# Sparse graph attention: units of at most four slots, stages one step apart, weighting on ScalarE

## The chip, the cores and the metric

One core of a Trainium2 chip. The metric is the device time of one execution in microseconds (us), median of several runs. All runs told here were in the fast state. A ratio is the mean time of one kernel's fast runs over the mean of the other's of the same rounds, so it is not quite the ratio of the medians that stand beside it. Engines: PE is TensorE, DVE is VectorE, ACT is ScalarE, POOL is GpSimd.

## The reference, cut to what matters

```python
# x (16, 1024, 512); adj (1024, 1024), a few neighbours per row; 8 heads of 64
h = maximum(layernorm(x), 0)
q, k, v = (h @ W + b for each of the three)          # (B, N, 8, 64)
scores  = einsum("bihd,bjhd->bhij", q, k) / sqrt(64) + where(adj == 0, -1e9, 0)
out     = x + einsum("bhij,bjhd->bihd", softmax(scores), v)
```

The adjacency is the same for all 16 batches and sparse, so the kernel makes lists of neighbours once. Rows are sorted by their number of neighbours; a tile is 128 sorted rows, and a tile of short rows needs few slots. Per slot, one indirect DMA gathers a neighbour's k and v for 128 rows (512 KB).

## The kernel before: what the argument touches

One "unit" is a few slots of one tile: (tile, first slot, slots). Tile -1 holds the overflow pieces of the longest rows.

```python
UNITS = ((7,0,2), (6,0,3), (5,0,4), (4,0,4), (3,0,5), (2,0,6), (1,0,4), (1,4,4), (0,0,6), (-1,0,5), (0,6,5))
gpool = pool("gpool", 3)                  # gathered units
ON_ACT, BY_REDUCE = (0, 1, 2), (5, 8, 9)  # weighted by ACT; summed over slots by DVE
# ... cut ...
def ahead(n):                             # one tile of projections, for the next batch
    if n + 3 < tiles: load_x(n + 3)       # indirect DMA, issued by POOL
    if n + 2 < tiles: stats(n + 2)        # DVE, with a power on POOL
    if n + 1 < tiles: flip(n + 1)         # PE transposes
    proj_kv(n)                            # 2 x 4 matmuls, bias on DVE, store
    if n + 2 < tiles: norm(n + 2)         # ACT
# ... cut: the loop over units i ...
    score(i)                              # DVE: k*q, reduce, mask; ACT: exp
    if i: weigh(i - 1)                    # DVE or ACT: v*w
    go_ahead(...)                         # some ahead(n)
    if new tile: queries(nb, nt)
    if i: add_up(i - 1)                   # PE: sum of the slots by identity matmuls
    if i + 2 < total: gather(i + 2)       # POOL
    # at a tile's end: finish(...)        # DVE: divide; POOL: + x, store
```

All four engines run in exactly the written order.

Of the kernel before, what the change touches and what calls it, by code (L numbers as in the profile page):

```python
# [38 lines left out]
CAPS = (11, 8, 6, 5, 4, 4, 3, 2)  # L39
PIECE = 5  # L40
PIECES = 17
LIST = CAPS[0] + PIECE * PIECES

UNITS = ((7, 0, 2), (6, 0, 3), (5, 0, 4), (4, 0, 4), (3, 0, 5), (2, 0, 6), (1, 0, 4), (1, 4, 4), (0, 0, 6), (-1, 0, 5), (0, 6, 5))
UMAX = max(n for _, _, n in UNITS)
SLOTS = sum(n for _, _, n in UNITS)


def main_path(tc, x, adj, Wq, bq, Wk, bk, Wv, bv, out, sums, cover):
# [11 lines left out]
    with ExitStack() as ctx:  # L61
        pool = lambda name, bufs=1, **k: ctx.enter_context(tc.tile_pool(name=name, bufs=bufs, **k))
        const = pool("const")
        xpool = pool("xpool", 14)
        hpool = pool("hpool", 2)
        htpool = pool("htpool", 12)
        kvpool = pool("kvpool", 3)
        gpool = pool("gpool", 3)
        work = pool("work", 2)
        small = pool("small", 4)  # L70
        wpool = pool("wpool", 3)
# [6 lines left out]
        ps_n = pool("ps_n", 1, space=psum)  # L78
# [12 lines left out]
        rows = gpool.tile([P, 5, N], F32, tag="g", name="rows")  # L91
        iota, key_row, rank_row, from_end, junk = (rows[:, k, :] for k in range(5))
# [97 lines left out]
        def proj_kv(n):  # L190
            b, t = tile_at(n)
            if b not in KV:
                KV[b] = dram.tile([N, 2 * D], F32, tag="kv", name=f"kv_{b}")
            kv = kvpool.tile([P, 2, D], F32, tag="kvt", name=f"kvt_{b}_{t}")
            for j, name in enumerate("kv"):
                pt = ps_kv.tile([P, D], F32, tag="pkv", name=f"p{name}_{b}_{t}")
                project(pt, name, n)
                nc.vector.tensor_tensor(kv[:, j, :], pt, bias[name], ALU.add)
            nc.sync.dma_start(KV[b][ts(t, P), :], kv.rearrange("p j d -> p (j d)"))
# [7 lines left out]
        for tile_, first, count in UNITS:  # L207
            first_col[tile_, first] = col
            col += count
# [10 lines left out]
        def make_lists():  # L220
            nc.vector.tensor_scalar(from_end, rank_row, -1.0, float(N), op0=ALU.mult, op1=ALU.add)
            adj_p = [adj_tile(f"adj_sorted_{g}") for g in range(NT // 4)]
            for t in range(NT):
                row = adj_p[t // 4][:, t % 4, :]
                nc.gpsimd.indirect_dma_start(out=row, out_offset=None, in_=adj, in_offset=on(ap=perm[:, t : t + 1], axis=0))
                nc.vector.scalar_tensor_tensor(row, row, 0.0, from_end, op0=ALU.not_equal, op1=ALU.mult)
                if t:
                    found = small.tile([P, 8], F32, tag="found", name=f"found_{t}")
                    nc.vector.max(found, row)
                    spread(t, found)  # L230

            row = adj_p[0][:, 0, :]
            found = const.tile([P, LIST + 1], F32, tag="found0", name="found_0")
            for k in range(LIST // 8):
                nc.vector.max(found[:, ts(k, 8)], row)
                if k < LIST // 8 - 1:
                    nc.vector.match_replace(row, found[:, ts(k, 8)], row, 0.0)
# [7 lines left out]
            before = ps_n.tile([P, 1], F32, tag="n", name="p_before")  # L245
# [12 lines left out]
            p_list = ps_n.tile([P, width], F32, tag="n", name="p_list")  # L258
# [24 lines left out]
        Q, G, WT, ACC = {}, {}, {}, {}  # L283

        def queries(b, t):
            pt = ps_q.tile([P, D], F32, tag="q", name=f"pq_{b}_{t}")
            if t >= 0:
                project(pt, "q", nth(b, t))
                HT.pop(nth(b, t))
            else:  # L290
                nc.tensor.matmul(pt, owner, Q[b, 0], start=True, stop=True)
                Q[b, t] = pt
                return
            if t == 0:
                q = Q[b, t] = work.tile([P, D], F32, tag="q0", name=f"q0_{b}")
            else:
                q = Q[b, t] = pt
            nc.vector.tensor_tensor(q, pt, bias["q"], ALU.add)

        def gather(i):  # L300
            b, u = divmod(i, NU)
            t, first, count = UNITS[u]
            c = first_col[t, first]
            G[i] = gpool.tile([P, UMAX, 2, D], F32, tag="g", name=f"g_{b}_{u}")
            for s in range(count):
                nc.gpsimd.indirect_dma_start(  # L306
                    out=G[i][:, s].rearrange("p j d -> p (j d)"),
                    out_offset=None,
                    in_=KV[b][:],
                    in_offset=on(ap=index[:, c + s : c + s + 1], axis=0),  # L310
                )

        def score(i):
            b, u = divmod(i, NU)
            t, first, count = UNITS[u]
            c = first_col[t, first]
            k = G[i][:, :count, 0, :]
            nc.vector.tensor_tensor(k, k, Q[b, t][:, None, :].to_broadcast([P, count, D]), ALU.mult)  # L318
            if first == 0:
                WT[b, t] = wpool.tile([P, CAPS[t] if t >= 0 else PIECE, H], F32, tag="w" if t else "w0", name=f"w_{b}_{t}")  # L320
            w = WT[b, t][:, first : first + count, :]
            nc.vector.tensor_reduce(w, k.rearrange("p s (h d) -> p s h d", h=H), AX.X, ALU.add)  # L322
            nc.vector.tensor_tensor(w, w, mask[:, c : c + count, None].to_broadcast([P, count, H]), ALU.add)  # L323
            nc.scalar.activation(w, w, AF.Exp, scale=HD**-0.5)  # L324

        ON_ACT = (0, 1, 2)

        def weigh(i):
            b, u = divmod(i, NU)
            t, first, count = UNITS[u]  # L330
            v = G[i][:, :count, 1, :].rearrange("p s (h d) -> p s h d", h=H)
            w = WT[b, t][:, first : first + count, :]
            if u in ON_ACT:
                for s in range(count):
                    for h in range(H):
                        nc.scalar.mul(v[:, s, h, :], v[:, s, h, :], w[:, s, h : h + 1])  # L336
            else:
                nc.vector.tensor_tensor(v, v, w[:, :, :, None].to_broadcast([P, count, H, HD]), ALU.mult)  # L338

        BY_REDUCE = (5, 8, 9)  # L340

        def add_up(i):

            b, u = divmod(i, NU)
            t, first, count = UNITS[u]
# [5 lines left out]
            acc = ACC[b, home]  # L351
            if u in BY_REDUCE:
                r = work.tile([P, D], F32, tag="r", name=f"r_{b}_{u}")
                nc.vector.tensor_reduce(r, v.rearrange("p s d -> p d s"), AX.X, ALU.add)  # L354
                terms = [r]
            else:
                terms = [v[:, s, :] for s in range(count)]
            for k, term in enumerate(terms):
                nc.tensor.matmul(  # L359
                    acc,  # L360
                    owner_t if t < 0 else ident,
                    term,
                    start=(u == units[0] and k == 0),
                    stop=(u == units[-1] and k == len(terms) - 1),
                )

        def finish(b, t):
            s = sums[:, b * NT + t, :]
            nc.vector.tensor_reduce(s, WT.pop((b, t)).rearrange("p s h -> p h s"), AX.X, ALU.add)  # L369
            if t == 0:  # L370
                more = small.tile([P, H], F32, tag="more", name=f"more_{b}")
                nc.vector.tensor_reduce(more, WT.pop((b, -1)).rearrange("p s h -> p h s"), AX.X, ALU.add)
                pt = ps_n.tile([P, H], F32, tag="n", name=f"p_more_{b}")
# [18 lines left out]
        tiles = B * NT  # L392
        done = [0]

        def ahead(n):

            if n + 3 < tiles:
                load_x(n + 3)
            if n + 2 < tiles:
                stats(n + 2)  # L400
            if n + 1 < tiles:
                flip(n + 1)
            proj_kv(n)
            if n + 2 < tiles:
                norm(n + 2)

        def go_ahead(target):
            while done[0] < min(tiles, target):
                ahead(done[0])
                done[0] += 1  # L410
# [3 lines left out]
        for n in range(min(2, tiles)):  # L414
            stats(n)
            norm(n)
        flip(0)
        make_lists()
        LEAD = 2
        with tc.manual_schedule(engines={mybir.EngineType.PE, mybir.EngineType.DVE, mybir.EngineType.Activation, mybir.EngineType.Pool}):  # L420
            go_ahead(NT + LEAD)
            total = B * NU
            gather(0)
            gather(1)
            queries(0, UNITS[0][0])
            passed = 0
            for i in range(total):
                b, u = divmod(i, NU)
                if u == 0:
                    passed = 0  # L430
                passed += UNITS[u][2]
                score(i)
                if i:
                    weigh(i - 1)
                go_ahead(NT * (b + 1) + LEAD + NT * passed // SLOTS)
                if i + 1 < total:
                    nb, nu = divmod(i + 1, NU)
                    nt = UNITS[nu][0]
                    if (nb, nt) not in Q:
                        queries(nb, nt)  # L440
                if i:
                    add_up(i - 1)
                if i + 2 < total:
                    gather(i + 2)
                if i:
                    pb, pu = divmod(i - 1, NU)
                    home = max(UNITS[pu][0], 0)
                    if pu == NU - 1 or max(UNITS[pu + 1][0], 0) != home:
                        finish(pb, home)
            weigh(total - 1)  # L450
            add_up(total - 1)
            finish(B - 1, 0)
# [188 lines left out]
```

## Time and profile before

| | before |
|---|---|
| time, median of 3 runs | 2871.07 us (2868.92 to 2874.26) |
| busy: PE, DVE, ACT, POOL | 72%, 75%, 17%, 51% |
| first multiply of the first batch | 194 us |
| one batch | 166.7 us |
| mean granted clock of PE | 0.866 |

```profile
DMA to landing us min/median/max: 3.3/4.6/7.4
```

POOL issues a load at 597.0; the statistics at 600.4 belong to the tile loaded one step earlier, and those at 631.0 are the first to read this load:

```profile
596.99 0.97 POOL L154 DMA_INDIRECT x<-in_x_dram,perm  x1 [0.30 <-issue]
```

```profile
600.36 0.69 DVE L163 BATCH_NORM_STATS2 st<-x 128x6 f32<-128x512 f32 x1
...
630.99 0.68 DVE L163 BATCH_NORM_STATS2 st<-x 128x6 f32<-128x512 f32 x1
```

### The profile page before, as it was taken

The page shows a single profiled execution, that of the slowest core. Times are in us where ns is not written, and L with a number is a line of the kernel's source. Part 1 is how long each engine was busy: PE and PEld are TensorE (multiplying, and loading weights), DVE is VectorE, ACT ScalarE, POOL GpSimd, SP SyncE. Part 2 cuts the span into 40 slices and gives each one's busy share as a digit, 9 for nine tenths or more (in the row PEclk, how much of TensorE's full clock was granted, in tenths as well). Part 3 has the DMA queues.
Part 4 walks back from the last instruction along what each step waited for, and adds up shares of the span by engine and source line. Part 5 has one row for each costly group of instructions (what it writes and reads, how often), then busy time and mean ns, then how long its engine had stood idle before and what let it go on. Part 6 is the DMA issues. An engine that isn't in the chain of part 4 may idle for free.

```text
span 2872.0 us, 16724 instructions
## 1 busy us (share of the span) xinstructions
PE 2074.3 (72%) x4759; PEld 912.0 (32%) x4759; DVE 2161.5 (75%) x2287; ACT 485.2 (17%) x1590; POOL 1462.3 (51%) x1298
## 2 busy tenths in 40 slices
PE   0587786876779687677968767796876779687552
PEld 0233332332334233233423323342332334233211
DVE  8447868687786868778687877878687777867766
ACT  0012030301203030120303012030301203020110
POOL 2125455464555546455554655455464645645452
PEclk9998898888989888888989888897988889798776
DMA  5146565564656556465655656565564656556452
GB/s 186 48 149 217 189 228 197 176 216 169 220 195 227 201 176 217 167 222 194 230 198 181 228 174 219 183 226 200 185 225 169 221 180 231 199 185 216 152 188 81
DMA packets 153922, 550.40 MB, mean 192 GB/s; under 512 B 18784, under 2 KB 18784, under 8 KB 153824
## 3 DMA queue, kind: packets, MB, share of 16 engines
q0 software_dynamic: 132224, 474.02, 49.3%
q1 hardware_dynamic: 21600, 75.24, 6.5%
q8 instruction: 40, 0.66, 0.1%
q14 instruction: 58, 0.48, 0.1%
HBM read 448.53 MB, written 100.66 MB: 191 GB/s over the span
## 4 chain that ended last, share of the span: by engine, by line
PE 43%; DVE 36%; issue 8%; ACT 6%; DMA 6%; POOL 1%; DVEq 0%; SPq 0%; ACTq 0%; POOLq 0%
PE acc L359 13%; PE pq L188 10%; PE pk L188 9%; PE pv L188 8%; DVE g L318 8%; DVE r L354 8%; DVE w L322 7%; DVE g L338 5%; ACT g L336 5%; DMA g<-kv,index 5%; PE pht L182 2%; DVE w L323 1%; POOL g L306 1%; DVE st L163 1%; ACT h L175 1%
## 5 line engine op out<-in xcount | busy, mean ns | idle before, releaser
L306 POOL DMA_INDIRECT g<-kv,index x768 | 865.9, 1127 | 988.1 <-PE acc L359 418.1
L359 PE MATMUL acc<-g,ident 128*128 128x512 f32 x992 | 500.4, 646 | 111.0 <-ACT g L336 64.5
L188 PE MATMUL pk<-wk,hT 128*128 128x512 f32 x1024 | 497.2, 631 | 0.0
L188 PE MATMUL pq<-wq,hT 128*128 128x512 f32 x1024 | 489.1, 623 | 0.0
L188 PE MATMUL pv<-wv,hT 128*128 128x512 f32 x1024 | 460.3, 592 | 0.0
L359 PE MATMUL acc<-r,ident 128*128 128x512 f32 x64 | 65.9, 1133 | 460.4 <-DVE sums L369 242.3
L322 DVE TENSOR_REDUCE w<-g 128x32 f32<-128x2048 f32 (+4 forms) x160 | 391.4, 2446 | 5.5
L359 PEld LDWEIGHTS acc<-g,ident 128*128 128x128 f32 x992 | 193.9, 203 | 388.7 <-issue 206.6
L338 DVE TENSOR_TENSOR g<-g,w 128x2048 f32<-128x2048 f32 (+2 forms) x112 | 306.9, 2740 | 0.0
L324 ACT ACTIVATE w<-w 128x32 f32<-128x32 f32 (+4 forms) x160 | 37.0, 231 | 1566.0 <-DVE w L323 1566.0
L318 DVE TENSOR_TENSOR g<-g,pq 128x2048 f32<-128x2048 f32 (+4 forms) x128 | 291.5, 2278 | 0.1
L188 PEld LDWEIGHTS pq<-wq,hT 128*128 128x128 f32 x1024 | 206.7, 203 | 265.7 <-issue 262.6
L336 ACT ACTIVATE g<-g,w 128x64 f32<-128x64 f32 x1152 | 280.0, 333 | 0.6 <-ACT w L324 0.2
L188 PEld LDWEIGHTS pv<-wv,hT 128*128 128x128 f32 x1024 | 194.6, 190 | 244.9 <-issue 241.3
L188 PEld LDWEIGHTS pk<-wk,hT 128*128 128x128 f32 x1024 | 204.3, 211 | 205.7 <-issue 205.7
L381 DVE TENSOR_TENSOR o<-acc,inv 128x512 f32<-128x512 f32 x128 | 88.6, 692 | 226.2 <-PE acc L359 223.8
L354 DVE TENSOR_REDUCE r<-g 128x512 f32<-128x3072 f32 (+1 forms) x48 | 241.9, 5039 | 0.6
L387 POOL DMA_INDIRECT out_dram<-o,perm x128 | 207.6, 1622 | 37.3 <-POOL o L386 35.3
L166 POOL TENSOR_TENSOR rstd<-rstd,minus_half 128x1 f32<-128x1 f32 x128 | 74.1, 579 | 259.2 <-DVE rstd L165 257.2
L175 ACT ACTIVATE h<-x,shift,rstd 128x512 f32<-128x512 f32 x128 | 104.0, 813 | 545.1 <-issue 439.7
L386 POOL TENSOR_TENSOR o<-o,x 128x512 f32<-128x512 f32 x128 | 164.6, 1286 | 37.5 <-DVE o L381 34.6
L359 PEld LDWEIGHTS acc<-r,ident 128*128 128x128 f32 x64 | 16.0, 311 | 486.3 <-issue 294.8
(218 smaller groups left out, 1415.3 us busy)
## 6 DMA issues: line engine op xcount, KB each, us to landing
kv<-kvt SPq DMA_DIRECT2D x128, 512.0 KB, 4.0
g<-kv,index POOLq DMA_INDIRECT x768, 5.7
adj<-in_adj_dram SPq DMA_DIRECT2D x8, 512.0 KB, 7.1
x<-in_x_dram,perm POOLq DMA_INDIRECT x128, 4.6
out_dram<-o,perm POOLq DMA_INDIRECT x128, 4.6
wk<-in_L_gnn_Wk_dram SPq DMA_DIRECT2D x1, 1024.0 KB, 11.7
wv<-in_L_gnn_Wv_dram SPq DMA_DIRECT2D x1, 1024.0 KB, 13.0
wq<-in_L_gnn_Wq_dram SPq DMA_DIRECT2D x1, 1024.0 KB, 12.4
```

What stands on the lines that cost most here:

```text
L175: nc.scalar.activation(HN[n], X[n], AF.Relu, bias=shift, scale=rstd)
L188: nc.tensor.matmul(pt, HT[n][:, c, :], W[name][:, c, :], start=(c == 0), stop=(c == DC - 1))
L306: nc.gpsimd.indirect_dma_start(out=G[i][:, s].rearrange("p j d -> p (j d)"), out_offset=None, in_=KV[b][:], in_offset=on(ap=index[:, c + s ...
L318: nc.vector.tensor_tensor(k, k, Q[b, t][:, None, :].to_broadcast([P, count, D]), ALU.mult)
L322: nc.vector.tensor_reduce(w, k.rearrange("p s (h d) -> p s h d", h=H), AX.X, ALU.add)
L336: nc.scalar.mul(v[:, s, h, :], v[:, s, h, :], w[:, s, h : h + 1])
L338: nc.vector.tensor_tensor(v, v, w[:, :, :, None].to_broadcast([P, count, H, HD]), ALU.mult)
L354: nc.vector.tensor_reduce(r, v.rearrange("p s d -> p d s"), AX.X, ALU.add)
L359: nc.tensor.matmul(acc, owner_t if t < 0 else ident, term, start=(u == units[0] and k == 0), stop=(u == units[-1] and k == len(terms) - 1),)
L381: nc.vector.tensor_mul(o.rearrange("p (h d) -> p h d", h=H), ACC.pop((b, t)).rearrange("p (h d) -> p h d", h=H), inv[:, :, None].to_broadc ...
L386: nc.gpsimd.tensor_tensor(o, o, X.pop(nth(b, t)), ALU.add)
L387: nc.gpsimd.indirect_dma_start(out=out_rows, out_offset=on(ap=perm[:, t : t + 1], axis=0), in_=o[:], in_offset=None, element_offset=b * N * D)
```

## The change

The intent: shorten DVE's work (no long reductions over slots, most of the weighting on ACT), and break the turn-taking between DVE and PE by smaller units, more buffers, and stages that lie one step apart. The core of the diff, with some lines joined:

```diff
+UNITS = ((7,0,2), (6,0,3), (5,0,4), (4,0,4), (3,0,3), (3,3,2), (2,0,3), (2,3,3), (1,0,4), (1,4,4),
+         (0,0,4), (-1,0,4), (0,4,4), (0,8,4))      # written in one column in the file
+BY_VECTOR = (10, 11, 12)
-        gpool = pool("gpool", 3)
+        gpool = pool("gpool", 5)
... cut: lists run beside the first projections; k and v halves of a tile apart ...
+        scores = ps_w.tile([P, SLOTS, H], F32, tag="w", name="scores")        # PSUM
+        weights = const.tile([P, SLOTS, H], F32, tag="weights", name="weights")
... cut: score(i) reduces into scores, adds the mask, exponential into weights, then ...
+            if i % NU in BY_VECTOR:
+                nc.scalar.activation(sc, sc, AF.Exp, scale=HD**-0.5)
+            else:
+                v = heads(G[i][:, :count, 1, :])
+                for s in range(count):
+                    for h in range(H):
+                        nc.scalar.activation(v[:, s, h, :], v[:, s, h, :], AF.Identity, scale=weights[:, c + s, h : h + 1])
+        def weigh(i):
+            if i % NU in BY_VECTOR:
+                nc.vector.tensor_tensor(heads(v), heads(v), scores[:, w, :, None]..., ALU.mult)
+            if count == 4 and b < B - 1:
+                nc.vector.tensor_tensor(v[:, 0:2], v[:, 0:2], v[:, 2:4], ALU.add)      # the pair addition
... cut ...
+        def pending(h):                      # h counts halves: n is the tile, j = 0 for k and 1 for v
+            n, j = divmod(h, 2)
+            before, after = [], []
+            if j == 0:
+                if n + 2 < tiles: before.append((stats, n + 2))
+                if n + 1 < tiles: before.append((flip, n + 1))
+            else:
+                if n + 3 < tiles: before.append((load_x, n + 3))
+                if n + 2 < tiles: after.append((norm, n + 2))
+            return before, after
... cut: the loop over units i ...
+                if i + 3 < total: gather(i + 3)
+                if i: weigh(i - 1)
+                for k, h in enumerate(todo):      # 0 to 2 halves of projections in a step
+                    before, after = pending(h)
+                    run(before); proj_kv(*divmod(h, 2))
+                    if k == 0: multiply(i)
+                    elif k == 1: score(i)
+                    store_kv(*divmod(h, 2)); run(after)
+                ...
+                if i: add_up(i - 1)
+                if len(todo) < 2: score(i)
+                ... bias of q; finish of the tile that ended one step earlier
```

## The prediction

> **What bounds the kernel now.** I read the page's busy times first, then the chain, then the stretches of one batch, the waits and the timeline.
>
> ```profile
> PE 2074.3 (72%) x4759; PEld 912.0 (32%) x4759; DVE 2161.5 (75%) x2287; ACT 485.2 (17%) x1590; POOL 1462.3 (51%) x1298
> ...
> PE 43%; DVE 36%; issue 8%; ACT 6%; DMA 6%; POOL 1%; DVEq 0%; SPq 0%; ACTq 0%; POOLq 0%
> ```
>
> No engine is full, and the chain passes between PE and DVE: they take turns. The table of stretches has busy time of PE, weight loads, DVE, ACT, POOL, then clock, DMA share, GB/s; one batch is this:
>
> ```profile
> 411.00:579.00 168.00, 127.68 (x291) 56.39 (x290) 127.34 (x133) 29.65 (x98) 91.32 (x79) 0.86 0.57 195
> ```
>
> DVE stands idle 41 us of a batch, PE 40, ACT 138; DMA is at 57%. The timeline of DVE gives the period, from the first multiply of a batch to the next:
>
> ```profile
> 194.25 1.22 DVE L318 TENSOR_TENSOR g<-g,pq 128x1024 f32<-128x1024 f32 x1
> ...
> 351.06 1.21 DVE L318 TENSOR_TENSOR g<-g,pq 128x1024 f32<-128x1024 f32 x1
> ...
> 2685.12 1.21 DVE L318 TENSOR_TENSOR g<-g,pq 128x1024 f32<-128x1024 f32 x1
> ```
>
> So: 194 us of preparation, a first batch of 157, then (2685.1-351.1)/14 = 166.7 each, and 187 for the last batch with the end. The waits say who takes turns (us, times, longest):
>
> ```profile
> PE acc L359 <- DVE r L354: 307.5, 32, 19.5
> ...
> PE acc L359 <- DVE sums L369: 242.3, 16, 15.2
> ...
> DVE o L381 <- PE acc L359: 223.8, 97, 8.0
> DVE shift L173 <- POOL rstd L166: 131.6, 75, 4.6
> ```
>
> PE waits 550 us for the long DVE reductions of units of 5 and 6 slots, DVE 224 for sums that PE makes late in the same step. One step in the timeline:
>
> ```profile
> 610.12 1.27 POOL L386 TENSOR_TENSOR o<-o,x 128x512 f32<-128x512 f32 x1
> 610.35 1.09 DVE L323 TENSOR_TENSOR w<-w,mask 128x32 f32<-128x32 f32 x1
> ...
> 614.75 5.33 DVE L354 TENSOR_REDUCE r<-g 128x512 f32<-128x3072 f32 x1
> ...
> 620.22 2.05 PE L359 MATMUL acc<-r,ident 128*128 128x512 f32 x2 [15.15 <-DVE sums L369]
> ...
> 622.91 5.11 PE L188 MATMUL pk<-wk,hT 128*128 128x512 f32 x8
> ...
> 627.86 3.60 PE L188 MATMUL pv<-wv,hT 128*128 128x512 f32 x8
> ```
>
> PE waits 15 us for the reduction and then runs its next group in 5.11 us rather than 3.60; the mask addition takes 1.09 us while POOL adds.
>
> **What the Trainium skill says.** "SBUF — State Buffer", Who interferes with whom: a DVE instruction with two SBUF inputs contends with a GpSimd instruction that reads SBUF, one with at most one such input doesn't. The trace agrees: the mask addition of 32 columns has a mean of 928 ns, the longer one of 48, beside which POOL rarely adds, 208. "TensorE: Matmul & The Clock Gate", What's actually happening: after an idle window of about 3.4 us PE runs at half clock until it has been busy as long. The trace agrees (5.11 against 3.60 above; mean clock 0.86). "ScalarE: Activation LUTs", What ACT_TABLE_LOAD costs: 186 ns + 0.833 per element + 93 for a pointer operand, with 93 overlapped: 239 ns for 64 elements with a pointer scale. Measured: 32 of them in 7.73 us, 242 each. "PSUM — Partial Sum Buffer", PSUM bank collisions: two engines must not be in one bank at a time. All scores now lie in one bank, and in the built order each score reduction waits for the exponential of the unit before.
>
> **The change part by part, per batch.** DVE now: multiplies 48 slots, 27.7 (2.28 for four, 1.75 for three, 1.21 for two); score reductions as much; mask 14 x 0.2 = 2.8; k/v bias 16 x 0.69 = 11.0; q bias 5.6; statistics 8 x 1.18 = 9.4; finishing 10.9. These stay. Removed: the three sums over slots (5.33+5.33+4.46 = 15.1) and the weighting of 39 slots on DVE, of which 12 stay (3 x 2.28 = 6.9 against 21.7 now). Added: eight additions of slot pairs, 1.21 each by the multiply of 1024 elements, 9.7. The mask stall goes (scores in PSUM leave one SBUF input): 64 x 0.73 = 47 us in 16 batches, 3. So DVE falls from 129 to about 112.
> ACT: weighting goes from 9 slots to 36, 288 x 0.242 = 69.6 instead of 17.4: about 85 busy in all.
> PE: 32 sums instead of 34, else the same: 24 groups of four projections x 3.44 = 82.6, 33 x 0.86 = 28, transposes 7: 118 at full clock.
> POOL and DMA: the same 48 gathers; five buffers, and gathers three units ahead instead of two, so the DMA wait of 3 us at each "-1" unit goes.
>
> If only DVE's work counted, a batch would take 120. But a unit of four is added in pairs only when ACT has weighted all four, and in the built order that addition stands first in the next step, ahead of the next multiply. From the end of the mask addition to the pair addition lie 0.25 (exponential) + 7.73 + 0.1 = 8.1 us; DVE has only bias, finishing or a store to put in between. I walk through one batch, DVE in its built order:
> Units 0 and 1 (two and three slots, no pair addition) wait for PE instead: pair addition of unit 13, two sums (3.4 after its cold gap), pv 5, q 3.4, sums of unit 0, then the small product for the last tile: finishing ends at 16.
> Unit 2: 1.0 statistics + 2.3 + 0.7 + 2.3 + 0.2 = 6.5, then q bias and finishing 2.1, then wait 6.0: its pair addition begins at 31.
> Unit 3: 1.2 + 2.3 + 0.8 + 2.3 + 0.2 + 8.1 (2.1 of it used) = 15: 46.
> Units 4 to 7, no pair addition: 8.0 + 4.7 + 7.4 + 9 (some of it waiting for pv and pk, as PE stood idle some 9 us until unit 3 was added): 75.
> Unit 8: multiply, two stores, statistics, reduction 8.2, wait 7.3 after the last store: 91.
> Unit 9: 15 again, wait 6.1: 106.
> Units 10, 11, 12, weighted by DVE, no wait for ACT: pair addition 1.2 + 7.3, then 3.5 (weighting and pair) + 8.7 with a finishing, 3.5 + 7.3, 3.5: 141 (PE keeps up).
> Unit 13: 1.0 + 2.3 + 0.7 + 2.3 + 0.2 + 8.1 = 14.6: 156 and round again.
> Of that DVE waits 33 us for ACT in five places and some 10 for PE.
>
> Preparation: lists run beside the projections of batch 0. DVE per tile: three list steps of 2.6, two stores, statistics, shift, and 1.2 of waiting for pk: 11.6, for 6.7 tiles, 9.3 after that. First tile at 65, +78 = 143, pieces 5, gather and landing 8: first multiply at 156 instead of 194.
> Batch 0 takes 23 halves of projections instead of 16 (PE +24, DVE +9): 165. Batches 1 to 13: 13 x 156 = 2028. Batch 14 runs out of projections in its last four units: 149. Batch 15 has no pair additions; the exponentials queue behind ACT's weighting (70 us), and three units on DVE follow: 105. The end, from the last finishing on: 16.5 as now.
> Sum: 156 + 165 + 2028 + 149 + 105 + 17 = 2620 us, 9% less.
>
> **The rivals.** (a) PE or DVE becomes the bound and the stages overlap as meant: a period of 120 to 135, 2110 to 2330 in all. For it: both have that little work. Against it: the built order puts DVE's pair addition behind ACT's 8 us, and DVE is in order. (b) The new waits eat everything: cold PE after each of the three long gaps, POOL delayed by two-input pair additions, waits for scores in their one bank: 165 or more a batch, 2740 and up. Against it: DVE loses 17 us of work, the 15 us reductions' waits on PE shrink to 9, and the exponentials in my walk come before the reductions that need them, except in the last batch. (c) DMA: 33 MB in 156 us is 215 GB/s, under the 230 that slices of the page show now, and a gather has some 30 us until it is used: hidden.
>
> **Range and chances.** One us of the period is 14 us in all. My walk may be off by 6 us in a period, as it has about a dozen hand-overs between engines of 0.1 to 0.2 that I rounded, and cold PE that I placed by hand; preparation and end by 20. So 2520 to 2710. Faster by over 2% (under 2814): 0.96; same: 0.03; slower: 0.01.
>
> **What would show it.** DVE waiting for ACT's weighting before the pair addition, 70 to 80 times by about 6 us, some 490 in all (33 x 15), as the longest wait of DVE; POOL's statistics wait and the DMA wait near zero; the mask addition at 0.2; DVE busy near 112 per batch, ACT near 85; PE still under full clock (0.85 to 0.92). First multiply near 156. If DVE's wait for ACT is small, the walk is wrong and (a) holds; if PE waits end most of DVE's idle time, (b).

## More of the kernel before

The waits for x in the kernel before (us, times, longest) are one line of 1.6 us; the view of the x tiles ends with the time from a load's issue to its landing:

```profile
DVE st L163 <- DMA x<-in_x_dram,perm: 1.6, 1, 1.6
```

## The result, and the profile after

The changed kernel takes 2900.02 us (median of 4 runs, 2896.84 to 2903.14), against 2872.27 of before in the same comparison: ratio 1.0098, 95% interval 1.008 to 1.0115. It is correct, and it is 1% slower. The prediction of 2620, with a range of 2520 to 2710, was wrong.

The page of the changed kernel, busy times and chain:

```profile
PE 2125.6 (73%) x4727; PEld 915.5 (32%) x4727; DVE 1772.4 (61%) x2426; ACT 1339.5 (46%) x5142; POOL 1345.2 (46%) x1298
...
DVE 22%; issue 22%; ACT 21%; POOL 17%; DMA 11%; PE 7%; POOLq 0%; DVEq 0%; SPq 0%; ACTq 0%
```

DVE has lost 389 us of work, and the time did not follow. The chain has new members: POOL had 1% of it and has 17%, DMA 6% and 11%. The stretch of one batch (columns as in the prediction):

```profile
1242.40:1415.40 173.00, 128.22 (x292) 55.75 (x292) 105.94 (x145) 83.39 (x321) 83.93 (x80) 0.88 0.56 195
```

DVE is busy 106 us of 173, where it was 127 of 168. The waits of DVE (us, times, longest):

```profile
DVE g L380 <- ACT g L372: 495.4, 75, 7.6
...
DVE st L179 <- DMA x<-in_x_dram,perm: 313.4, 50, 12.3
...
DVE kvt L219 <- PE pv L204: 97.6, 45, 3.5
...
DVE shift L189 <- POOL rstd L182: 4.2, 3, 2.7
```

The first line is the wait that was predicted, at the size predicted: 75 times, 495 us. The second is new, and no step of the prediction has it: the statistics wait 313 us for x. In the stretch 1242 to 1415 it is 22.7 us. (POOL's loads of x, for their part, have no wait for a free buffer of more than 0.3 us in this kernel, so a lack of x buffers is not the reason.)

What happens there, POOL's timeline (start, duration, engine, line, operation, idle time before and what ended it):

```profile
1295.50 1.06 POOL L423 DMA_INDIRECT out_dram<-o,perm  x1 [0.29 <-POOL o L422]
1296.86 0.96 POOL L348 DMA_INDIRECT g<-kv,index  x1 [0.30 <-ACT g L372]
...
1301.59 1.28 POOL L422 TENSOR_TENSOR o<-o,x 128x512 f32<-128x512 f32 x1
1303.15 1.01 POOL L423 DMA_INDIRECT out_dram<-o,perm  x1 [0.28 <-POOL o L422]
1304.47 0.96 POOL L348 DMA_INDIRECT g<-kv,index  x1 [0.30 <-issue]
...
1309.47 0.95 POOL L170 DMA_INDIRECT x<-in_x_dram,perm  x1 [0.30 <-issue]
```

and DVE's beside it:

```profile
1305.73 0.19 DVE L364 TENSOR_TENSOR scores<-scores,mask 128x24 f32<-128x24 f32 x1
1316.94 0.69 DVE L179 BATCH_NORM_STATS2 st<-x 128x6 f32<-128x512 f32 x1 [11.02 <-DMA x<-in_x_dram,perm]
...
1337.85 0.69 DVE L179 BATCH_NORM_STATS2 st<-x 128x6 f32<-128x512 f32 x1 [10.80 <-DMA x<-in_x_dram,perm]
```

From 1295 on POOL works with pauses of 0.3 us only: stores, gathers of two units, an addition. The load of x stands behind all of it, is issued at 1309.5 and lands 7.5 us later; DVE, in its own order, stands at the statistics and can do nothing else. The same happens again 21 us later, and in the next batch at 1488 (9.6 us) and 1509 (10.7 us).

The time in pieces, from the starts of the batches in DVE's timeline (each batch begins with the first multiply of 1024 elements):

```profile
163.60 1.22 DVE L358 TENSOR_TENSOR g<-g,pq 128x1024 f32<-128x1024 f32 x1 [3.96 <-DMA g<-kv,index]
...
373.81 1.22 DVE L358 TENSOR_TENSOR g<-g,pq 128x1024 f32<-128x1024 f32 x1
...
2627.21 1.22 DVE L358 TENSOR_TENSOR g<-g,pq 128x1024 f32<-128x1024 f32 x1
...
2771.26 1.21 DVE L358 TENSOR_TENSOR g<-g,pq 128x1024 f32<-128x1024 f32 x1
```

| | predicted | changed | off by |
|---|---|---|---|
| until the first batch | 156 | 163.6 | +8 |
| batch 0 | 165 | 210.2 | +45 |
| batches 1 to 13 | 13 x 156 | 13 x 173.3 | +225 |
| batch 14 | 149 | 144.1 | -5 |
| batch 15 and the end | 122 | 126.3 | +4 |
| sum | 2620 | 2897.6 | +277 |

So 270 of the 277 us lie in batches 0 to 13, and the waits for x are 313 us.

### The profile page after: what moved, and what is told of

The parts are those of the page before. It is cut to its first block, busy times and chain, and to the rows that moved or that the text cites. A ratio compares the mean times of both kernels' runs of the same rounds, so it can differ in the third digit from the quotient of the medians.

```text
span 2897.6 us, 20683 instructions
## 1 busy us (share of the span) xinstructions
PE 2125.6 (73%) x4727; PEld 915.5 (32%) x4727; DVE 1772.4 (61%) x2426; ACT 1339.5 (46%) x5142; POOL 1345.2 (46%) x1298
## 4 chain that ended last, share of the span: by engine, by line
DVE 22%; issue 22%; ACT 21%; POOL 17%; DMA 11%; PE 7%; POOLq 0%; DVEq 0%; SPq 0%; ACTq 0%
ACT g L372 20%; POOL g L348 11%; DMA x<-in_x_dram,perm 10%; DVE scores L363 7%; DVE g L358 3%; PE acc L393 3%; DVE g L380 3%; DVE kvt L219 2%; POOL o L422 2%; DVE st L179 2%; POOL out_dram L423 2%; PE pv L204 2%; PE pk L204 1%; DMA g<-kv,index 1%; DVE g L378 1%
## 5 line engine op out<-in xcount | busy, mean ns | idle before, releaser
L372 ACT ACTIVATE g<-g,weights 128x64 f32<-128x64 f32 x4608 | 1119.9, 333 | 11.4 <-issue 3.6
L348 POOL DMA_INDIRECT g<-kv,index x768 | 776.5, 1011 | 415.7 <-issue 218.7
L393 PE MATMUL acc<-g,ident 128*128 128x512 f32 x988 | 574.9, 711 | 391.1 <-DVE g L380 245.8
L422 POOL TENSOR_TENSOR o<-o,x 128x512 f32<-128x512 f32 x128 | 164.3, 1284 | 708.3 <-DVE o L417 707.0
L380 DVE TENSOR_TENSOR g<-g 128x1024 f32<-128x1024 f32 x120 | 147.0, 1225 | 496.9 <-ACT g L372 495.4
L363 DVE TENSOR_REDUCE scores<-g 128x32 f32<-128x2048 f32 (+2 forms) x224 | 444.0, 1982 | 5.9 <-ACT weights L365 2.8
L198 PE MATMUL pht<-ident,h 128*128 128x128 f32 x512 | 101.3, 330 | 326.2 <-ACT h L191 319.9
L179 DVE BATCH_NORM_STATS2 st<-x 128x6 f32<-128x512 f32 x128 | 88.3, 690 | 345.9 <-DMA x<-in_x_dram,perm 313.4
L358 DVE TENSOR_TENSOR g<-g,pq 128x2048 f32<-128x2048 f32 (+2 forms) x160 | 296.9, 1856 | 4.7 <-DMA g<-kv,index 4.0
L170 POOL DMA_INDIRECT x<-in_x_dram,perm x128 | 129.9, 1015 | 71.5 <-DVE perm L155 39.3
L423 POOL DMA_INDIRECT out_dram<-o,perm x128 | 132.3, 1033 | 36.3 <-POOL o L422 33.5
```

The costliest lines, as they stand in the source:

```text
L179: nc.vector.bn_stats(st, X[n])
L198: nc.tensor.transpose(pt[:, c, :], hn[:, ts(c, P)], ident)
L348: nc.gpsimd.indirect_dma_start(out=G[i][:, s].rearrange("p j d -> p (j d)"), out_offset=None, in_=KV[b][:], in_offset=on(ap=index[:, c + s ...
L358: nc.vector.tensor_tensor(k, k, Q[b, t][:, None, :].to_broadcast([P, count, D]), ALU.mult)
L363: nc.vector.tensor_reduce(sc, heads(G[i][:, :count, 0, :]), AX.X, ALU.add)
L372: nc.scalar.activation(v[:, s, h, :], v[:, s, h, :], AF.Identity, scale=weights[:, c + s, h : h + 1])
```

## The experiments

The indented text under each edit is what I expected of that run before it was built.

Theory after the result: the changed kernel loads x for tile n+3 in the second half of tile n and reads it in the first half of tile n+1, which is the next half and sometimes the same step; before, a whole tile lay between. Take that away and the prediction's walk holds, about 2620 us. Rival: the wait for x only hides others (cold PE, ACT), and little is won.

### x a tile earlier

```diff
-        xpool = pool("xpool", 16)
+        xpool = pool("xpool", 17)
-                if n + 3 < tiles:
-                    before.append((load_x, n + 3))
+                if n + 4 < tiles:
+                    before.append((load_x, n + 4))
-        for n in range(min(3, tiles)):
+        for n in range(min(4, tiles)):
```

> The changed kernel with each x tile loaded one tile (two halves) earlier, and a 17th x buffer for it. Theory 1 (the x tile is asked for only half a step before its statistics, behind four to eight gathers in POOL's queue, and DVE waits some 10 us for it in units 7 and 8): the 313 us wait of the statistics for x goes below 30, the period falls from 174 to 154-157, the time to 2580-2640, which is my walk as predicted. Theory 2 (the wait for x is only where another limit shows: POOL's queue of gathers, or PE, sets the pace): another wait of DVE takes its place, and the time stays over 2800.

Measured 2607.22 us (2603.67 to 2608.17), ratio to before 0.9068 (0.9053 to 0.9083). Waits, and one batch:

```profile
DVE g L380 <- ACT g L372: 467.1, 75, 7.6
...
DVE st L179 <- DMA x<-in_x_dram,perm: 3.8, 1, 3.8
```

```profile
1265.50:1419.10 153.60, 126.32 (x292) 54.98 (x292) 106.08 (x145) 83.38 (x321) 84.32 (x80) 0.92 0.64 219
```

The wait for x went from 313 to 4 us and the time fell by 293. The work of a batch is unchanged (DVE 106.1, ACT 83.4); only its period is 153.6 instead of 173. The predicted 156 was the period of a kernel whose x comes in time. The rival falls.

### The load ahead of the gathers, half a tile early as in the change

Is it the distance, or the place in POOL's queue? Here the loads of a step stand ahead of its gathers, nothing else is different:

```diff
+                for h in todo:
+                    if h % 2 and h // 2 + 3 < tiles:
+                        load_x(h // 2 + 3)
                 if i + 3 < total:
                     gather(i + 3)
...
-                    run(before)
+                    run([c for c in before if c[0] is not load_x])
```

> The changed kernel with the x load put ahead of the gathers of its own step in POOL's queue, at the same step and with the same buffers. Theory 1: it is issued some 5 us sooner and its packets do not queue behind one unit's gathers, so about half of the wait for x (21 us a batch) goes: 2700-2790. If what delays it is the traffic of the DMA engines rather than its place in the queue, little changes: over 2850.

Measured 2681.57 us (2678.3 to 2685.7), ratio 0.9334 (0.9319 to 0.935), somewhat better than expected. The wait for x:

```profile
DVE st L179 <- DMA x<-in_x_dram,perm: 131.7, 32, 6.1
```

So 182 of the 313 us of waiting belong to the place behind the gathers of the load's own step (four of them at 1304.5 to 1309.2 above, 5 us). The rest is what stands in the queue from the step before and the short distance itself; this run does not separate these two.

### The kernel before, robbed of its distance

```diff
-            if n + 3 < tiles:
-                load_x(n + 3)
+            if n + 2 < tiles:
+                load_x(n + 2)
             if n + 2 < tiles:
                 stats(n + 2)
```

(Two loads instead of three are made at the start.)

> The kernel before, with each tile's x loaded in the same tile's step as its statistics, instead of one tile earlier. Theory: the distance from the load to the statistics in the order of POOL's queue is what the changed kernel lost; the kernel before, robbed of it too, waits 5 to 12 us at each of some 120 tiles, less what DVE's own idle 41 us a batch take up: 3100 to 3900 us, and a wait of DVE's statistics for x of 600 us or more. Rival: the wait for x belongs to the new order alone: within 2% of 2872 us.

Measured 3094.1 us (3090.05 to 3099.56), ratio 1.0775 (1.0757 to 1.0793). The time is just under the range and the wait is smaller than expected:

```profile
DVE st L163 <- DMA x<-in_x_dram,perm: 472.3, 104, 7.3
```

That is 4.5 us each, not 5 to 12: little more than a landing, which took 3.2 to 5.4 us in this run (median 3.8). There the load goes out nearly in time, and mostly its landing is no longer hidden. Of 472 us, 223 reach the time (3094 less 2871). The rival ("within 2%") falls: the old order hid x only by its distance.

### The pair addition later, with and without x a tile earlier

With x in time, DVE still waits 467 us for ACT before the pair addition. So I put weighting and pair addition behind the score of the next unit:

```diff
                 if i + 3 < total:
                     gather(i + 3)
-                if i:
-                    weigh(i - 1)
...
-                if i:
-                    add_up(i - 1)
                 if len(todo) < 2:
                     score(i)
+                if i:
+                    weigh(i - 1)
+                    add_up(i - 1)
```

Alone, with x as in the change:

> The changed kernel with the weighting and pair addition of the unit before placed after the score of the present unit rather than ahead of its multiply; x loads as they are. ACT then has some 9 us of DVE work to hide its 8.1 us behind. Theory 1: the 495 us wait for ACT's weighting falls below 80, but the x waits stay or grow a little, as x is asked for no sooner: 2400-2560. If the waits for ACT were hidden behind the x waits, it would gain next to nothing: over 2800.

Measured 2823.36 us (2816.77 to 2827.11), ratio 0.9827 (0.9811 to 0.9844): a miss. The wait for ACT did fall (495 to 45 us), but the wait for x grew:

```profile
DVE st L179 <- DMA x<-in_x_dram,perm: 455.6, 79, 12.1
```

With x a tile earlier too:

> Both edits: x a tile earlier and the pair addition after the score. Theory 1: neither wait is left, a batch takes 125-140 as PE (118 at full clock and cold spells) and DVE (112) overlap, 2150-2350 in all. Theory 2: POOL's or PE's queue keeps the period above 150: over 2500.

Measured 2595.29 us (2594.01 to 2596.24), ratio 0.9029 (0.9014 to 0.9044): a plain miss, only 12 us better than x a tile earlier alone. The waits of this second one show where the gain went:

```profile
DVE kvt L219 <- PE pk L204: 256.1, 112, 7.6
PE acc L393 <- DVE g L380: 250.8, 73, 6.7
...
DVE kvt L219 <- PE pv L204: 192.5, 120, 3.1
DVE pq L342 <- PE pq L204: 126.5, 77, 4.5
DVE g L380 <- ACT g L372: 13.5, 15, 1.0
```

The wait for ACT is gone (467 to 13.5), and DVE now waits 575 us for PE's projections, where it waited 257 with x a tile earlier alone. One handover in its timeline:

```profile
1366.98 1.22 DVE L380 TENSOR_TENSOR g<-g 128x1024 f32<-128x1024 f32 x1
...
1368.25 3.78 PE L393 MATMUL acc<-g,ident 128*128 128x512 f32 x4 [3.98 <-DVE g L380]
...
1371.83 1.72 PE L335 MATMUL pq_-1_7391<-q,owner 128*128 128x512 f32 x2
...
1373.59 2.29 DVE L358 TENSOR_TENSOR g<-g,pq_-1_7391 128x2048 f32<-128x2048 f32 x1 [4.38 <-PE pq_-1_7391 L335]
```

The pair addition is now at the end of DVE's step, and PE's sums, which need it, stand ahead of PE's next product. PE waits 4 us for DVE, then DVE 4.4 us for PE. I had moved one end of a dependence and not the other. That the wait for x grew in the first of the two fits DVE no longer having the wait for ACT in which x could arrive; no run tests this.

### PE's sums a step later too

```diff
 # on top of the second kernel above
-                if i + 3 < total:
-                    gather(i + 3)          # at the start of the step
...
-                    add_up(i - 1)          # behind weigh(i - 1)
+                if i > 1:                  # ahead of score(i), where the sums stood in the change
+                    add_up(i - 2)
+                if i + 3 < total:
+                    gather(i + 3)
```

(A tile is finished a step later accordingly.)

> x a tile earlier, the pair addition behind the score of the next unit, and PE's sums one step later still (with the gather into that buffer behind them). Theory: with the pair addition put later the loss came back because PE's sums stood before its next projections and waited for DVE's pair addition; with the sums a step later neither DVE waits for ScalarE nor PE for the pair addition: a period of 135 to 150, 2250 to 2480 us. Rival: what holds DVE is PE's own amount of work at a clock below full, or gathers that are now issued later: 2540 us or more.

Measured 2159.14 us (2154.75 to 2161.18), ratio 0.7514 (0.7501 to 0.7526). Better than the range that I gave. Page, one batch, waits:

```profile
PE 1926.5 (89%) x4727; PEld 857.5 (40%) x4727; DVE 1795.0 (83%) x2426; ACT 1334.8 (62%) x5142; POOL 1373.8 (64%) x1298
```

```profile
1186.80:1310.00 123.20, 117.49 (x294) 52.74 (x293) 107.10 (x145) 83.27 (x323) 85.57 (x81) 0.99 0.79 273
```

```profile
DVE kvt L219 <- PE pk L204: 125.6, 70, 7.3
...
PE acc L393 <- DVE g L380: 34.4, 17, 4.8
...
DVE g L380 <- ACT g L372: 14.5, 16, 1.0
```

The work of a batch is that of the changed kernel, on every engine; its period is 123.2 us instead of 173. PE is busy 95% of it. As PE no longer stands idle, its clock is 0.99 instead of 0.88 and the same matmuls take 117.5 us instead of 128.2, which none of my expectations had counted.

### No pair addition where ACT weighs

The other way out: PE sums all four slots of those units, DVE has nothing to wait for (x a tile earlier).

```diff
-            if count == 4 and b < B - 1:
+            if i % NU in BY_VECTOR and b < B - 1:
                 ... pair addition
-            count = 2 if count == 4 and b < B - 1 else count
+            count = 2 if u in BY_VECTOR and b < B - 1 else count
```

> x loaded a tile earlier, and the pair addition taken away from the units that ScalarE weighs (their four sums all go to PE, after its projections). Theory: the 467 us that DVE waits for ScalarE with x ahead came from the pair addition's place in DVE's order, and PE's sums, which stand behind 3.5 to 14 us of projections in PE's order, hardly wait for ScalarE themselves. Then DVE loses that wait and 6 us a batch of work, PE gets 9 us a batch more: a period of about 140 to 150, 2350 to 2480 us in all. Rival: the turn-taking only changes hands, PE waits for ScalarE and DVE for PE's projections, as when the pair addition was put later: 2560 to 2620.

Measured 2273.19 us (2272.5 to 2273.93), ratio 0.7916 (0.7903 to 0.7929); again better than the range, again with a high clock (0.979). DVE has five pair additions less in a batch and PE ten more sums, so PE has more work than before, and yet 334 us are won (2607 to 2273). DVE's busy time fell by only 74 us (1775.5 to 1701.3): most of what cost the time was where DVE stood and waited, not how much there was to do.

### The last order without the x load's distance

The kernel with the sums a step later, and x loaded as in the change (16 buffers, n+3, three at the start).

> The order of the run with the sums a step later, but x loaded as in the changed kernel, half a tile ahead of its statistics. Theory: the load's lateness is a fault of its own, which the order of the pair addition and the sums doesn't mend: a wait of DVE's statistics for x of 250 to 500 us and 2350 to 2600 us in all, against 2159 with x a tile earlier. Rival: x came late only because everything before it in POOL's queue was held up by the turn-taking; with that gone it comes in time: under 2230 us, and a wait for x under 80.

Measured 2383.48 us (2379.74 to 2385.55), ratio 0.8295 (0.8282 to 0.8308):

```profile
DVE st L179 <- DMA x<-in_x_dram,perm: 339.3, 61, 10.2
```

The load's lateness is a fault of its own. POOL's queue shows why the rival fails. In the changed kernel POOL waits 707 us (109 times) for DVE's finishing before its own addition, with later gathers and loads standing behind that; here it waits 55 us (32 times) for it, and x is late all the same.

One thing in this run is not as in the change, and the expectation does not mention it: the gathers moved behind the projections together with the sums, so a load now stands ahead of the gathers of its own step, as in the second experiment. What stands before it are the gathers and stores of earlier steps: POOL works from 1207.9 on without a longer pause than 0.3 us before it issues a load at 1229.4, and DVE waits 7.6 us for that load. So the last row of this table of medians (us) is not in every respect a repeat of the first two:

| order | x as in the change | x a tile earlier | difference |
|---|---|---|---|
| as in the change | 2900 | 2607 | 293 |
| pair addition later | 2823 | 2595 | 228 |
| and sums a step later | 2383 | 2159 | 224 |

### Scores in SBUF

The prediction gave 47 us to "scores in PSUM leave one SBUF input". Undone, on top of x a tile earlier:

```diff
-        scores = ps_w.tile([P, SLOTS, H], F32, tag="w", name="scores")
+        scores = const.tile([P, SLOTS, H], F32, tag="scores", name="scores")
```

(Three small buffers were made single to find the room.)

> x a tile earlier, scores in SBUF instead of PSUM (three small buffers made single to find the room). Theory: mask additions of 32 columns go from 0.2 us back to 0.9 where POOL adds beside them; if each of the eight in a batch were met, that is 8 x 0.73 x 16 = 93 us of DVE time, half of it on the path that sets the end: 2630 to 2700 us against 2607. Rival: the addition falls where POOL seldom adds, or into DVE's waits: 2590 to 2620 us.

Measured 2610.47 us (2609.43 to 2611.16), ratio 0.909 (0.9074 to 0.9105); 2607 with PSUM. The row of its mask addition (busy, mean ns):

```profile
L363 DVE TENSOR_TENSOR scores<-scores,mask 128x32 f32<-128x32 f32 x128 | 25.5, 200 | 4.4
```

200 ns in SBUF too: the rival. I counted in the timelines how many 32-column mask additions overlap an addition of POOL's: 48 of 64 before (1.15 us each; the other sixteen 0.25), one of 128 here (1.06 us), none in the changed kernel. The new order takes them apart; in it PSUM has nothing left to save. (In the fastest order, with the sums a step later, 13 of the 128 meet an addition of POOL's again, and with the scores in PSUM they take 0.2 us; what SBUF would cost there was not run.)

### Scores in PSUM in the kernel before

So that PSUM's part is measured where the two do meet:

```diff
-            nc.vector.tensor_reduce(w, k..., AX.X, ALU.add)
-            nc.vector.tensor_tensor(w, w, mask..., ALU.add)
-            nc.scalar.activation(w, w, AF.Exp, scale=HD**-0.5)
+            sc = scores[:, c : c + count, :]          # PSUM
+            nc.vector.tensor_reduce(sc, k..., AX.X, ALU.add)
+            nc.vector.tensor_tensor(sc, sc, mask..., ALU.add)
+            nc.scalar.activation(w, sc, AF.Exp, scale=HD**-0.5)
```

> The kernel before with its scores in PSUM, nothing else of the change (the small products move to the buffer of the transposes to free a bank). There 62 of 160 mask additions, counted in the timelines, stand beside an addition of POOL's and take 1.15 to 1.30 us instead of 0.2. Theory: with one SBUF input left they take 0.2 us there too; DVE loses 62 x 1.0 = 62 us of busy time, of which perhaps half lies on the path: 2825 to 2855 us against 2872, the mean of the 32-column addition 0.2 us. Rival: it is the neighbourhood alone, whatever the memory: the mean stays near 0.9 us, and the time within 5 us of 2872.

Measured 2846.13 us (2837.79 to 2850.88), ratio 0.9904 (0.9889 to 0.992). Mask addition and weighting of four slots in this kernel:

```profile
L325 DVE TENSOR_TENSOR scores<-scores,mask 128x32 f32<-128x32 f32 x64 | 12.8, 200 | 2.2
...
L340 DVE TENSOR_TENSOR g<-g,w 128x2048 f32<-128x2048 f32 x48 | 125.2, 2609 | 0.0
```

and the weighting in the kernel before:

```profile
L338 DVE TENSOR_TENSOR g<-g,w 128x2048 f32<-128x2048 f32 x48 | 109.6, 2283 | 0.0
```

All 48 still overlap POOL's addition and take 0.2 us: the stall is real and PSUM takes it away. But DVE's busy time fell by 31 us (2161.5 to 2130.1), not 62: the weighting comes next, has two SBUF inputs, and now meets POOL's addition itself (48 x 0.33 us here, and 32 x 0.41 in the units of six, 29 us together).

### More pair sums on DVE

The best kernel with two slots added on DVE in the units of two and three slots as well:

```diff
+            elif b < B - 1:
+                nc.vector.tensor_tensor(v[:, 0], v[:, 0], v[:, count - 1], ALU.add)
...
-            count = 2 if count == 4 and b < B - 1 else count
+            count = (count + 1) // 2 if b < B - 1 else count
```

> The run with x ahead and the sums a step later, with two slots added on DVE in the units of two and three slots too. That run had PE busy 95% and DVE 87% of a stretch in the middle. Theory: PE's amount of work bounds it now; six additions of 512 columns cost DVE some 4 us a batch and take six passes off PE, by its 607 ns each 3.6 us: 14 x 3.6 = 50 us, and with their weight loads up to 80: 2080 to 2115 us. Rival: DVE or the waits between the two bind as much: 2140 to 2190 us.

Measured 2192.61 us (2191.99 to 2193.91), ratio 0.7634 (0.7624 to 0.7645): slower than 2159, the theory's miss and just above the rival's range. The added row:

```profile
L382 DVE TENSOR_TENSOR g<-g 128x512 f32<-128x512 f32 x90 | 82.5, 917 | 14.2 <-ACT g L372 14.2
```

917 ns each, 82 us in this row (DVE's busy time in all rose by 63, 1795.0 to 1857.7) for 50 us of PE (1926.5 to 1876.8): 29 of the 90 overlap an addition of POOL's and take 1.41 us, the others 0.68. At 87% and 95%, work could not be shifted between the two for nothing. What the 33 us that were lost consist of was not followed further.

## Why the prediction was wrong

**The step that failed.** It is the walk's "Units 4 to 7, no pair addition: 8.0 + 4.7 + 7.4 + 9 ... : 75" and "Unit 8: ... wait 7.3 after the last store: 91", together with rival (c), "a gather has some 30 us until it is used: hidden". I had asked of DMA only whether the gathers are hidden, and they are (4.0 us of DVE waiting for them in the whole kernel). The load of x is a DMA too, on the same POOL queue, and the change had cut its lead from a tile to half a tile and placed it behind the gathers. Set against the walk from its start at 1414.2 (the pair addition of unit 13), the trace has the pair addition of unit 2 at 30.1 (walk: 31), of unit 3 at 44.6 (46), units 4, 5 and 6 take 7.7, 4.6 and 7.5; then units 7 and 8 wait for x, 9.6 and 10.7 us, which the walk doesn't have. The sign "the DMA wait near zero" fails with it. A batch had 22 us of such waits; the period was 173.3 instead of 156. With x a tile earlier it is 153.6.

**What was right.** DVE waits for ACT 75 times, 495 us (predicted 70 to 80 times, 490). The mask addition takes 0.2 us, the statistics' wait for POOL's power fell from 132 to 4 us, DVE is busy 106 us a batch (112), ACT 83 (85), the clock is 0.874 (0.85 to 0.92). The 112 adds up durations; taken from the 129 by its own differences it would be 106. In the stretch of one batch DVE's durations add up to 111.2 us, but neighbouring instructions overlap and the busy time is 105.9. (The 239 ns of an ACT instruction is an estimate from the page named there; the walk uses the measured 242.) Of the rivals, (a) holds for the last order but not for the change: 123.2 us a period, within its 120 to 135. (b), 165 us or more a batch, came true in its size by luck: none of its three causes is x, and the trace shows little of them. Score reductions wait 2.8 us for exponentials in the whole kernel, POOL's additions take 1284 ns (1286 before), and the clock is in the range of the walk.

**Sizes that were off.** Batch 0 was predicted at 165 and took 210.2. With x in time it takes 182.7, so x is 27 of the 45 us and the other 18 are a size that was wrong: with x in time DVE still waits there 24 us for ACT and 43 for pk, pv and pq, and I had added only work for the seven extra halves (PE 24, DVE 9). The regular period was too long by 2.4 us, 31 in thirteen batches, so that these two partly cancel in 2607 against 2620. The first multiply came at 163.6, not 156; why was not looked into.

**A right number for a wrong reason.** The mask stall did go, but by the order, not by PSUM, as the two runs on scores show; and where PSUM does it, half of the stall moves to the next instruction with two SBUF inputs. "SBUF — State Buffer" of the Trainium skill, section Who interferes with whom, holds in both; I applied it to the instruction and did not ask whether the two would still meet.

**Where my expectations failed later.** For the pair addition put later I expected DVE's wait for ACT to be simply won. It came back as a wait of PE for DVE and of DVE for PE, until the sums moved by a step as well.

What is not settled: why the wait for x costs 293 us in one order and 224 in another (in the last order the load also stands ahead of its step's gathers); and whether the best order has a better split between DVE and PE than the one tried.

## What to carry to other kernels

When a change reorders a loop, list for every load and every hand-over how far its producer stands ahead of its consumer, before and after, counted in the in-order queue that issues it; a transfer that showed no wait before can lose its lead without any line of it being changed in substance. When one end of a dependence between two in-order engines is moved by a step, move the other end too, or the wait only changes its owner. A stall that depends on two instructions meeting in time is removed or moved by order as well as by memory, so check in the new order whether they still meet.

## What the Trainium skill lacked or had wrong

- "DMA: Bandwidth & Descriptors", section Anatomy of one DMA — SWDGE (gpsimd) path: its fit, 2.0 us and the bytes at 436 GB/s, gives an estimate of 2.6 us for one load of x (256 KB). In the kernel before an indirect load of x took 3.3 to 7.4 us from issue to landing, median 4.6, with gathers beside it; the late one shown of the changed kernel took 7.5. For indirect loads in a busy queue the fit is too short.
- The same page has no figure for how long a load stands behind other work in POOL's order before it is issued: in the changed kernel POOL worked from 1295.5 to 1309.5 us on stores, gathers (0.95 us and a pause of 0.3 each) and an addition before it issued the load. Putting the loads ahead of the gathers of their own step was worth 218 us of 2900.
- "SBUF — State Buffer", section Who interferes with whom: right in kind (a mask addition with two SBUF inputs took 1.15 us beside POOL's addition, with one 0.2). It does not say that taking the stall from one instruction hands it to the next: of 61 us taken from the mask additions 29 came back in the weighting.
- "TensorE: Matmul & The Clock Gate", section What's actually happening: the trace agrees that PE slows after gaps. The page works out such a loss for a loop that waits for DMA (section HAM oscillation — how this bites in real kernels). What this case adds is a loop whose gaps come from the order of two engines: the same 292 to 294 matmul instructions of one batch took 128.2 us at a clock of 0.88 and 117.5 at 0.99, so that removing gaps returned 11 us of PE's own work besides the gaps.
